# Last stage of a two-layer graph attention kernel: float32 sums per 32-node quarter in place of 128-node sums with partly split rows

## The chip, the cores and the metric

One core of a Trainium2 chip runs the whole kernel. Its engines work side by side: TensorE (PE, with weight loads shown apart as PEld), VectorE (DVE), ScalarE (ACT), GpSimd (POOL) and SyncE (SP). Each takes its own instructions in order and waits for the others by semaphores. The metric is device time in microseconds, the median of several runs. Beside it there is one profiled execution, from which all durations come.

## What is computed

Two layers of a relational graph attention network on 3125 nodes and 53125 edges, then a residual sum and a layer norm. Edges come sorted by destination. One layer, with its max taken per destination node:

```python
xr = jnp.einsum('nd,rdf->rnf', x, W)
oi = xr[etype, dst]
oj = xr[etype, src]
alpha = jax.nn.leaky_relu(oi @ q + oj @ k, NEG_SLOPE)
m = jax.ops.segment_max(alpha, dst, num_segments=n_nodes)
e = jnp.exp(alpha - m[dst])
z = jax.ops.segment_sum(e, dst, num_segments=n_nodes)
a = e / (z[dst] + EPS)
msg = (a[:, :, None] * oj.reshape(-1, heads, out_ch)).reshape(-1, heads * out_ch)
out = jax.ops.segment_sum(msg, dst, num_segments=n_nodes)
```

Layer 1 has 4 heads, layer 2 has one; rows are 768 wide. Between the layers stands an ELU; at the end `_layernorm(x + out)`. The change is in the last stage, the edge part of layer 2 with the layer norm: for each node, the sum of its edges' rows, each times its weight p = exp(alpha - m), divided by the sum of the p.

## The kernel before

A first stage makes layer 1's tables of node rows, a second does layer 1's edges and layer 2's dense products, and the last, `phase3` (L1015), layer 2's edges.

**Blocks and slots.** Edges are taken in blocks of at most 128 consecutive destination nodes and at most 2176 edges, 25 blocks (NB) in all. A block's edges lie in 17 slots (SL) of 128 edges, one edge per partition; the first block has 14 (SLF). That makes NK = 422 slots. Since edges are sorted, the edges of slot j of a block belong to a narrow stretch of its nodes, about 7.5 nodes wide, at a place near 7.5 j.

**One slot.** `gather(k)` (L1031) has POOL issue one indirect DMA (L461) that brings the 128 edges' source rows of 772 float32 into place k mod NG of the tile G; NG is 36. Column 768 and on of a row carry the constant 1 (which makes the sum of p) and the score part. `high(k)` and `low(k)` (L1134, L1151) prepare the operands of PE, `sums(k)` (L1160) adds the slot into `acc`, a PSUM tile of two halves of 386 columns, one per block, 128 nodes on the partitions.

There are two kinds of slots, chosen by `whole(k)` (L1126). A whole slot's weights of PE are `selp`, 128 edges by 128 nodes, with p where the edge goes to the node: ACT makes it in two operations (L1141, L1142), and two float32 matmuls, one per half, multiply it with the gathered rows. In the other slots ACT makes H, the rows times p rounded to the format float32r (L1146), DVE makes L, what is left (L1157), and `sel` of ones and zeros (L1148); four float32r matmuls add H and L. 281 slots are whole and 141 are split. In the last 17 slots (`late`) one of three is whole, and `sel` is made on POOL.

**Weights p of a block.** When all its rows are there: `a_alpha` (L1081) on DVE adds the scores; PE transposes them (L1098); DVE scans for the maximum of each node (L1104, L1106) and subtracts (L1109); ACT takes exp (L1113); PE transposes back (L1117); DVE puts p and its negative np in place (L1122, L1124). Ahead of this, PE spreads the block's destinations over partitions (bc, L1050), ACT copies them (sT, L1056), DVE compares (L1060, L1062), and PE picks the destinations' scores (pq, L1071).

**Order.** The program's order on every engine is written out by hand: a loop over steps k issues `gather(k)`, then `sums(k - 28)` (LAG = SL + 11), then what `ev` holds for the step, then `low(k - 26)` and `high(k - 25)`. So the sums of a block begin when its own 17 gathers and 11 more have been issued. Counted from the step of a block's first gather, `a_alpha` stands at step 19, the transposes at 20 and 23, `a_put` at 24. The end of a block (`e_y` to `e_out`, L1171 to L1217) divides, norms and stores its rows.

**Flag.** The second half of the program, a slower kernel, runs only if `flag` (L594, L1292) is not zero, which tells of inputs that the blocks can't hold. `bad` collects such cases.

Of the kernel before, what the change touches and what calls it, by code (L numbers as in the profile page):

```python
# [8 lines left out]
F32 = mybir.dt.float32  # L9
F32R = mybir.dt.float32r  # L10
# [3 lines left out]
AF = mybir.ActivationFunctionType  # L14
ALU = mybir.AluOpType
AX = mybir.AxisListType
# [4 lines left out]
P = 128  # L21
# [16 lines left out]
SL = 17  # L38
# [4 lines left out]
FRONT = 256  # L43
BACK = CAP + P + 256

WHOLE = (17, 25)


@with_exitstack
def kernel(  # L50
# [23 lines left out]
    NB = (N + P - 1) // P  # L74
# [3 lines left out]
    l1, l2 = layers  # L78
    H1 = l1["H"]
    F1 = D // H1  # L80
# [3 lines left out]
    RW = D + 4  # L84
    HW = RW // 2
    CW = F1 + 1
    LL = FRONT + E + BACK
    NK = (NB - 1) * SL + SLF
    V, S, G, T = nc.vector, nc.scalar, nc.gpsimd, nc.tensor
# [17 lines left out]
    row = keep.tile([P, P], F32, name="frow")  # L107
# [3 lines left out]
    rel3 = keep.tile([P, R, 3], F32, name="rel3")  # L111
# [6 lines left out]
    n_all = keep.tile([P, NB + 1], F32, name="n_all")  # L118
# [6 lines left out]
    bad = keep.tile([1, 2], F32, name="bad")  # L125
    oidx = keep.tile([P, 1], I32, name="oidx")
    flag = keep.tile([1, 1], I32, name="flag")
    ridx = keep.tile([P, NB, SL], I32, name="ridx")
    rfirst = keep.tile([P, len(first_rows), SL], I32, name="rfirst")
    dl = keep.tile([P, NB, SL + 1], F32, name="fdl")  # L130
# [311 lines left out]
    def base(b):  # L442

        return SLF + (b - 1) * SL if b else 0

    def slots(b):
        return SL if b else SLF

    def slot(k):

        return divmod(k - SLF + SL, SL) if k >= SLF else (0, k)

    ends = {base(b) + slots(b) - 1 for b in range(NB)}
# [65 lines left out]
    def phase1(pre, work, psum, wH, wL, qq):  # L519
# [7 lines left out]
        st = a_st  # L527
# [58 lines left out]
        def a_last():  # L586

            V.tensor_scalar(oidx, n_all[:, NB - 1:NB], col, None, op0=ALU.add)
            V.tensor_scalar(starts[0:1, 2, :NB], n_all[0:1, :NB], float(N - P), None, op0=ALU.min)
            more = work.tile([1, 2], F32, name="more", bufs=1)  # L590
            V.tensor_single_scalar(more[:, 0:1], n_all[0:1, NB:NB + 1], float(N), op=ALU.is_lt)
            V.tensor_single_scalar(more[:, 1:2], n_all[0:1, NB - 2:NB - 1], float(N - P), op=ALU.is_gt)
            V.tensor_add(bad, bad, more)
            V.tensor_add(flag, bad[:, 0:1], bad[:, 1:2])  # L594

        def a_gather(b, j):
            gathered[b, j] = gather_rows(kts[b % 3][:, j, :], kt1, b, j).ins
# [197 lines left out]
        for n in range(max(ev) + 1):  # L795
            for f, b in ev.get(n, ()):
                f(b)
            b, i = divmod(n, 6)
# [26 lines left out]
    def phase2(work, psum, wH, wL):  # L825
# [3 lines left out]
        gs = share  # L829
        NG = len(gs)  # L830
        rows = [work.tile([P, RW], F32, name=f"r2_{i}", bufs=1) for i in range(3)]
# [183 lines left out]
    def phase3(work, psum):  # L1015
        for i in range(2):
            xbs.append(work.tile([P, D], F32, name=f"xb3_{i}", bufs=1))
            x_load3(len(xbs) - 1)
        NG = 36
        gs = work.tile([P, NG, RW], F32, name="G", bufs=1)  # L1020
        als = [work.tile([P, SL + 2], F32, name=f"al2_{i}", bufs=1) for i in range(2)]
        for t in als:
# [1 line left out]
        blk = {}  # L1024
        st = {}
# [97 lines left out]
            s["np"] = work.tile([P, SL], F32, name="np2", bufs=3)  # L1123
            V.tensor_scalar(s["np"], s["pa"][:, 3 * P:3 * P + SL], -1.0, None, op0=ALU.mult)  # L1124

        def whole(k):  # L1126

            return k % 3 == 0 if late(k) else k * WHOLE[0] % WHOLE[1] < WHOLE[0]

        def late(k):  # L1130

            return k >= NK - SL

        def high(k):  # L1134
            b, j = slot(k)
            g = gs[:, k % NG, :]
            p = blk[b]["p"][:, j:j + 1]
            if whole(k):
                sel = work.tile([P, P], F32, name="selp", bufs=4)

                S.activation(sel, row, AF.Abs, bias=dl[:, b, j:j + 1], scale=-1.0)  # L1141
                S.activation(sel, sel, AF.Relu, bias=p, scale=blk[b]["np"][:, j:j + 1])  # L1142
                st[k] = [sel, g]
                return
            H = work.tile([P, RW], F32R, name="H", bufs=4)
            S.activation(H, g, AF.Copy, scale=p)  # L1146
            sel = work.tile([P, P], F32R, name="sel", bufs=4)
            (G if late(k) else V).tensor_scalar(sel, row, dl[:, b, j:j + 1], None, op0=ALU.is_equal)  # L1148
            st[k] = [sel, H]

        def low(k):  # L1151
            if whole(k):
                return
            b, j = slot(k)
            g = gs[:, k % NG, :]
            L = work.tile([P, RW], F32R, name="L", bufs=3)
            V.scalar_tensor_tensor(L, g, blk[b]["p"][:, j:j + 1], st[k][1].bitcast(F32), op0=ALU.mult, op1=ALU.subtract)  # L1157
            st[k].append(L)

        def sums(k):  # L1160
            b, j = slot(k)
            sel, *parts = st.pop(k)
            if j == 0:
                blk[b]["acc"] = psum.tile([P, 2, 512], F32, name="acc", bufs=2)
            acc = blk[b]["acc"]
            for i, a in enumerate(parts):
                for c in range(2):
                    T.matmul(acc[:, c, :HW], sel, a[:, c * HW:(c + 1) * HW], start=(j == 0 and i == 0),  # L1168
                             stop=(k in ends and i == len(parts) - 1))

        def e_y(b):  # L1171
            s = blk[b]
# [51 lines left out]
        LAG = SL + 11  # L1224
# [14 lines left out]
        for k in range(max(ev) + 1):  # L1239
            if k < NK:  # L1240
                gather(k)
            if 0 <= k - LAG < NK:
                sums(k - LAG)
            for f, a in ev.get(k, []):
                f(*a)
            if 0 <= k - LAG + 2 < NK:
                low(k - LAG + 2)
            if 0 <= k - LAG + 3 < NK:
                high(k - LAG + 3)

    with tc.manual_schedule():
        with tc.tile_pool(name="share", bufs=1) as pool:
# [4 lines left out]
            with tc.tile_pool(name="wbuf", bufs=1) as wbuf:  # L1257
                wH = wbuf.tile([P, R * DT, D + 2], F32R, name="wH")
                wL = wbuf.tile([P, R * DT, D + 2], F32R, name="wL")
                with tc.tile_pool(name="pre", bufs=1) as pre:  # L1260
                    qq = pre.tile([P, NB, H1, R], F32, name="qq")
                    with tc.tile_pool(name="work0", bufs=1) as work, tc.tile_pool(
                        name="psum0", bufs=1, space=PSUM
# [20 lines left out]
                    with tc.tile_pool(name="work1", bufs=1) as work, tc.tile_pool(  # L1284
                        name="psum1", bufs=1, space=PSUM
# [544 lines left out]
```

## Time and profile before

| what | value |
|---|---|
| median of three timed runs | 2547.97 us (2543.3 to 2552.66) |
| profiled execution, its own time | 2188.15 us |
| its span | 2186.4 us |
| mean granted clock of PE | 0.969 |
| PE busy, share of the span | 2015.1 us, 92% |
| POOL busy | 1674.3 us, 77% |
| DVE busy | 1458.8 us, 67% |
| ACT busy | 1356.5 us, 62% |
| first gather of the last stage | 1552.1 us |
| end of the last stage's gathers | 2147.6 us |
| end of its last matmul | 2174.2 us |

Times in a profile are counted from the start of the span. A group of instructions is given as line, engine, operation, tile written and tiles read, shapes and count, then busy time and mean of one in ns, then the idle time just before them on their engine and what ended most of it. A float32 matmul of the program shows up as two pairs of a weight load and a matmul instruction, a float32r matmul as one. Matmuls are pipelined, so the duration of one contains its latency; what it costs is the distance to the next.

### The profile page before, as it was taken

How to read it: one execution, taken by the hardware profiler on the slowest of the kernel's cores; microseconds unless marked ns; L12 is line 12 of the kernel's file. 1: busy time of each engine (PE TensorE's matmuls, PEld its weight loads, DVE VectorE, ACT ScalarE, POOL GpSimd, SP SyncE). 2: the span in 40 equal slices, each digit the busy share in tenths (PEclk: the TensorE clock that was granted, in tenths of full speed). 3: DMA queues.
4: the chain of work that ended last, by engine and by line, in shares of the span. 5: the costliest groups of instructions: out<-in, count | busy, mean ns of one | idle time of the engine just before them, and what ended most of it. 6: DMA issues, size and time to landing. Idle time of an engine off the chain costs nothing.

```text
span 2186.4 us, 37632 instructions
## 1 busy us (share of the span) xinstructions
PE 2015.1 (92%) x10953; PEld 1730.7 (79%) x10953; DVE 1458.8 (67%) x4031; ACT 1356.5 (62%) x3159; POOL 1674.3 (77%) x1615
## 2 busy tenths in 40 slices
PE   5979999999987799999999999999499999989997
PEld 5979998899887799999999999999355555555555
DVE  6535554454534899999999999998155555556555
ACT  5412111122111788888888888887268887878786
POOL 4257777777777888888888888886477777777774
PEclk9989999999998899999999999999799999999999
DMA  6555545545457977888787878786789998988883
GB/s 177 188 137 173 192 145 169 174 158 183 160 168 224 311 233 246 240 246 241 237 249 226 249 231 248 231 243 191 256 303 305 315 322 309 302 295 281 294 300 108
DMA packets 156842, 506.04 MB, mean 231 GB/s; under 512 B 43875, under 2 KB 57069, under 8 KB 156628
## 3 DMA queue, kind: packets, MB, share of 16 engines
q0 software_dynamic: 81904, 331.52, 49.9%
q1 hardware_dynamic: 64494, 156.04, 20.6%
q10 hardware_dynamic: 10230, 15.98, 2.2%
q8 instruction: 91, 1.49, 0.3%
q14 instruction: 123, 1.01, 0.2%
HBM read 412.55 MB, written 95.69 MB: 232 GB/s over the span
## 4 chain that ended last, share of the span: by engine, by line
PE 61%; POOL 12%; DMA 11%; issue 11%; DVE 3%; ACT 1%; POOLq 0%; SPq 0%; DVEq 0%; ACTq 0%
PE po L949 19%; PE acc L1168 14%; PE acc L894 12%; PE po L698 8%; POOL kt L461 8%; DMA G<-ftab,ridx 6%; POOL G L461 2%; DMA kt<-kt,ridx 1%; POOL share L461 1%; PE bank L282 1%; DVE L L875 1%; PE pt L260 1%; POOL sel L863 1%; PE pt L924 1%; PE po L396 1%
## 5 line engine op out<-in xcount | busy, mean ns | idle before, releaser
L861 ACT ACTIVATE H<-share,pall 128x193 fp32r<-128x193 f32 x1672 | 618.2, 447 | 104.7 <-PE acc L894 53.5
L875 DVE SCALAR_TENSOR_TENSOR L<-share,pall,H 128x193 fp32r<-128x193 f32 x1672 | 619.0, 435 | 28.2 <-issue 19.8
L949 PE MATMUL po<-wH,hT 128*128 128x386 f32 (+1 forms) x1800 | 529.1, 339 | 0.0
L461 POOL DMA_INDIRECT G<-ftab,ridx x374 | 416.0, 1112 | 113.9 <-issue 56.1
L461 POOL DMA_INDIRECT share<-ftab,ridx x374 | 437.0, 1168 | 80.4 <-DVE L L875 34.7
L461 POOL DMA_INDIRECT kt<-kt,ridx x374 | 396.3, 1060 | 114.0 <-issue 108.5
L698 PE MATMUL po<-wH,xT 128*128 128x384 f32 x1584 | 440.3, 348 | 8.8 <-ACT share L713 4.4
L1168 PE MATMUL acc<-G,selp 128*128 128x386 f32 x1124 | 417.1, 505 | 0.0
L949 PEld LDWEIGHTS po<-wH,hT 128*128 128x128 f32 x1800 | 334.1, 189 | 0.6 <-DVE hT L937 0.5
L698 PEld LDWEIGHTS po<-wH,xT 128*128 128x128 f32 x1584 | 294.6, 191 | 13.8 <-ACT share L713 6.2
L949 PE MATMUL po<-wL,hT 128*128 128x386 f32 (+1 forms) x900 | 304.8, 339 | 0.0
L1168 PEld LDWEIGHTS acc<-G,selp 128*128 128x128 f32 x1124 | 206.0, 193 | 118.7 <-issue 16.3
L698 PE MATMUL po<-wL,xT 128*128 128x384 f32 x792 | 270.3, 341 | 0.0
L894 PE MATMUL acc<-H,sel 128*128 128x386 f32 x836 | 227.0, 353 | 19.2 <-POOL sel L863 17.6
L713 ACT COPY share<-po 128x384 f32<-128x384 f32 x144 | 67.9, 478 | 275.0 <-PE po L698 268.9
L863 POOL TENSOR_SCALAR sel<-frow,fdl 128x128 fp32r<-128x128 f32 x278 | 219.0, 788 | 12.4 <-PE acc L894 1.7
L894 PE MATMUL acc<-L,sel 128*128 128x386 f32 x836 | 217.8, 342 | 0.0
L1157 DVE SCALAR_TENSOR_TENSOR L<-G,p,H 128x772 fp32r<-128x772 f32 x141 | 143.1, 1017 | 56.1 <-ACT H L1146 56.0
L894 PEld LDWEIGHTS acc<-H,sel 128*128 128x128 f32 x836 | 148.0, 190 | 36.0 <-POOL sel L863 33.7
L949 PEld LDWEIGHTS po<-wL,hT 128*128 128x128 f32 x900 | 169.6, 188 | 0.0
L894 PEld LDWEIGHTS acc<-L,sel 128*128 128x128 f32 x836 | 155.1, 191 | 0.2 <-DVE L L875 0.2
L698 PEld LDWEIGHTS po<-wL,xT 128*128 128x128 f32 x792 | 151.8, 192 | 0.0
(246 smaller groups left out, 2688.1 us busy)
## 6 DMA issues: line engine op xcount, KB each, us to landing
ftab<-share SPq DMA_DIRECT2D x75, 386.0 KB
ftab<-r SPq DMA_DIRECT2D x75, 386.0 KB
share<-in_L_gnn_W_dram SPq DMA_DIRECT2D x36, 384.0 KB
w_d<-w2hl SPq DMA_DIRECT2D x18, 768.0 KB
sT<-dr_d SPq DMA_DIRECT2D x25, 544.0 KB
share<-in_x_dram SPq DMA_DIRECT2D x25, 384.0 KB
xb_d<-share SPq DMA_DIRECT2D x25, 384.0 KB
xr<-in_x_dram SPq DMA_DIRECT2D x23, 384.0 KB
```

Of the source, the lines that this page charges most:

```text
L260: T.transpose(pt[:, f, c * P:(c + 1) * P], a[:, (2 * i + f) * P:(2 * i + f + 1) * P], ident)
L282: T.matmul(to, a[:, 2 * i + f, :], t[:, f, :w], start=(n == 0), stop=(n == 2 * DT - 1))
L461: return G.indirect_dma_start(out=to, out_offset=None, in_=tab, in_offset=_index(i[:, j:j + 1]), bounds_check=NP * R - 1, oob_is_err=False)
L698: m = T.matmul(po[:, :HALF], xT[:, s, t, :], w[:, i, sl], start=(n == 0), stop=(n == 3 * DT - 1))
L713: S.copy(to, po[:, :HALF].rearrange("p (h f) -> p h f", h=2))
L861: S.activation(H[:, c], g[:, c], AF.Copy, scale=pall[:, b, j, h:h + 1])
L863: (V if k % 3 == 0 else G).tensor_scalar(sel, row, dl[:, b, j:j + 1], None, op0=ALU.is_equal)
L875: V.scalar_tensor_tensor(L[:, c], g[:, c], pall[:, b, j, h:h + 1], H[:, c].bitcast(F32), op0=ALU.mult, op1=ALU.subtract)
L894: T.matmul(acc[:, c, :HW], sel, a[:, c * HW:(c + 1) * HW], start=(j == 0 and i == 0), stop=(k in ends2 and i == 1), skip_group_check=True)
L949: T.matmul(po[:, :wd], hT[:, k, t, :], w[:, r * DT + t, sl], start=(t == 0 and n == 0), stop=(t == DT - 1 and n == 2))
L1157: V.scalar_tensor_tensor(L, g, blk[b]["p"][:, j:j + 1], st[k][1].bitcast(F32), op0=ALU.mult, op1=ALU.subtract)
L1168: T.matmul(acc[:, c, :HW], sel, a[:, c * HW:(c + 1) * HW], start=(j == 0 and i == 0), stop=(k in ends and i == len(parts) - 1))
```

## The change

The block's 128 nodes are four quarters of 32. For each of the 17 slots a table `WINDOW` names the one or two quarters in which its edges' nodes lie (seven slots have one, ten have two). All slots are treated alike: `selp` is made for those 32 or 64 nodes alone, and each pair of slot and quarter t gets its own two float32 matmuls (one per half), with 32 weight columns, into partitions 32t to 32t+31 of `acc`. H, L, `sel` and `low` are gone.

Slots are taken in the order of `ROUNDS`, seven groups of two or three slots. A round's matmuls are issued together when its last slot's turn comes, half by half, quarter after quarter. `in_turn` maps steps to this order; gathers keep theirs. In the last 17 slots every other `selp` is made by one DVE operation in place of two of ACT's. NG is 43 in place of 36, and `selp` has 10 buffers in place of 4.

A new function `windows`, at step 17, tests on DVE (and with one small matmul) whether every edge of a block lies in its slot's window, and adds the count of those outside to `bad`; `flag` is set there and no longer in `a_last`.

```diff
-WHOLE = (17, 25)
+WINDOW = ((0,), (0,), (0,), (0, 1), (0, 1), (0, 1), (1,), (1, 2), (1, 2), (1, 2), (2,), (2, 3), (2, 3), (2, 3),
+          (2, 3), (3,), (3,))
+ROUNDS = ((3, 11), (4, 12), (5, 13), (2, 9), (0, 7, 15), (1, 8, 16), (6, 14, 10))
...
-        NG = 36
+        NG = 43
...
+        def in_turn(k):
+            b, i = slot(k)
+            o = [j for r in ROUNDS for j in r if j < slots(b)]
+            return b, o[i]
...
         def high(k):
-            b, j = slot(k)
-            g = gs[:, k % NG, :]
+            b, j = in_turn(k)
             p = blk[b]["p"][:, j:j + 1]
-            if whole(k):
-                sel = work.tile([P, P], F32, name="selp", bufs=4)
-                S.activation(sel, row, AF.Abs, bias=dl[:, b, j:j + 1], scale=-1.0)
+            lo, hi = WINDOW[j][0] * 32, WINDOW[j][-1] * 32 + 32
+            sel = work.tile([P, 64], F32, name="selp", bufs=10)[:, :hi - lo]
+            if late(k) and k % 2:
+                V.tensor_scalar(sel, row[:, lo:hi], dl[:, b, j:j + 1], p, op0=ALU.is_equal, op1=ALU.mult)
+            else:
+                S.activation(sel, row[:, lo:hi], AF.Abs, bias=dl[:, b, j:j + 1], scale=-1.0)
                 S.activation(sel, sel, AF.Relu, bias=p, scale=blk[b]["np"][:, j:j + 1])
-                st[k] = [sel, g]
+            st[b, j] = sel
+
+        def sums(k):
+            b, j = in_turn(k)
+            n = slots(b)
+            if not any(j == [i for i in r if i < n][-1] for r in ROUNDS):
                 return
-            H = work.tile([P, RW], F32R, name="H", bufs=4)
-            S.activation(H, g, AF.Copy, scale=p)
-            sel = work.tile([P, P], F32R, name="sel", bufs=4)
-            (G if late(k) else V).tensor_scalar(sel, row, dl[:, b, j:j + 1], None, op0=ALU.is_equal)
-            st[k] = [sel, H]
-
-        def low(k):
...
+            o = [(i, t) for r in ROUNDS for i in r if i < n for t in WINDOW[i]]
+            now = [(i, t) for i, t in o if i in next(r for r in ROUNDS if j in r)]
+            for c in range(2):
+                for i, t in now:
+                    u = [x for x, y in o if y == t]
+                    T.matmul(acc[32 * t:32 * t + 32, c, :HW], st[b, i][:, 32 * (t - WINDOW[i][0]):][:, :32],
+                             gs[:, (base(b) + i) % NG, c * HW:(c + 1) * HW], start=(i == u[0]), stop=(i == u[-1]))
+            for i, t in now:
+                st.pop((b, i), None)
+
+        def windows():
+            lim = work.tile([P, 2, SL], F32, name="lim", bufs=1)
+            for j in range(SL):
+                V.memset(lim[:, 0, j:j + 1], 32.0 * WINDOW[j][0])
+                V.memset(lim[:, 1, j:j + 1], 32.0 * WINDOW[j][-1] + 32.0)
...
+            V.tensor_tensor(v[0], d, lim[:, 0, None, :].to_broadcast([P, NB, SL]), op=ALU.is_ge)
+            V.tensor_tensor(v[1], d, lim[:, 1, None, :].to_broadcast([P, NB, SL]), op=ALU.is_lt)
+            V.tensor_mul(v[0], v[0], v[1])
...
+            V.tensor_reduce(out_, v[1].rearrange("p b j -> p (b j)"), AX.X, ALU.add)
+            po = psum.tile([P, 512], F32, name="bc", bufs=2)
+            T.matmul(po[:1, :1], out_, rel3[:, 1, 0:1], start=True, stop=True)
...
-            if 0 <= k - LAG + 2 < NK:
-                low(k - LAG + 2)
+            if k == SL:
+                windows()
             if 0 <= k - LAG + 3 < NK:
                 high(k - LAG + 3)
```

More of the change, by code (lines that the diff above doesn't have):

```diff
@@ L593, in a_last @@
             V.tensor_add(bad, bad, more)
-            V.tensor_add(flag, bad[:, 0:1], bad[:, 1:2])
         def a_gather(b, j):
@@ L1124, in a_put @@
             V.tensor_scalar(s["np"], s["pa"][:, 3 * P:3 * P + SL], -1.0, None, op0=ALU.mult)
-        def whole(k):
-            return k % 3 == 0 if late(k) else k * WHOLE[0] % WHOLE[1] < WHOLE[0]
         def late(k):
             return k >= NK - SL
+        def in_turn(k):
+            b, i = slot(k)
+            o = [j for r in ROUNDS for j in r if j < slots(b)]
+            return b, o[i]
         def high(k):
-            b, j = slot(k)
-            g = gs[:, k % NG, :]
+            b, j = in_turn(k)
@@ L1148, in high @@
-            (G if late(k) else V).tensor_scalar(sel, row, dl[:, b, j:j + 1], None, op0=ALU.is_equal)
-            st[k] = [sel, H]
-        def low(k):
[L1152 to L1163, printed above, removed]
+            lo, hi = WINDOW[j][0] * 32, WINDOW[j][-1] * 32 + 32
@@ new lines, in high @@
+            sel = work.tile([P, 64], F32, name="selp", bufs=10)[:, :hi - lo]
[3 more added lines that the diff above has]
+                S.activation(sel, row[:, lo:hi], AF.Abs, bias=dl[:, b, j:j + 1], scale=-1.0)
+                S.activation(sel, sel, AF.Relu, bias=p, scale=blk[b]["np"][:, j:j + 1])
+            st[b, j] = sel
[3 more added lines that the diff above has]
+            if not any(j == [i for i in r if i < n][-1] for r in ROUNDS):
+                return
+            if "acc" not in blk[b]:
@@ L1164, in sums @@
                 blk[b]["acc"] = psum.tile([P, 2, 512], F32, name="acc", bufs=2)
             acc = blk[b]["acc"]
[L1166 to L1169, printed above, removed]
+            o = [(i, t) for r in ROUNDS for i in r if i < n for t in WINDOW[i]]
+            now = [(i, t) for i, t in o if i in next(r for r in ROUNDS if j in r)]
@@ new lines, in sums @@
+            for c in range(2):
[10 more added lines that the diff above has]
+                V.memset(lim[:, 1, j:j + 1], 32.0 * WINDOW[j][-1] + 32.0)
+            own = work.tile([P, NB], F32, name="own3", bufs=1)
+            V.tensor_sub(own, n_all[:, 1:NB + 1], n_all[:, :NB])
+            v = [work.tile([P, NB, SL], F32, name=f"v{i}", bufs=1) for i in range(2)]
+            d = dl[:, :, :SL]
+            V.tensor_tensor(v[0], d, lim[:, 0, None, :].to_broadcast([P, NB, SL]), op=ALU.is_ge)
+            V.tensor_tensor(v[1], d, lim[:, 1, None, :].to_broadcast([P, NB, SL]), op=ALU.is_lt)
+            V.tensor_mul(v[0], v[0], v[1])
+            V.tensor_tensor(v[1], d, own[:, :, None].to_broadcast([P, NB, SL]), op=ALU.is_lt)
+            V.tensor_tensor(v[1], v[1], v[0], op=ALU.is_gt)
+            out_ = work.tile([P, 1], F32, name="outside", bufs=1)
+            V.tensor_reduce(out_, v[1].rearrange("p b j -> p (b j)"), AX.X, ALU.add)
+            po = psum.tile([P, 512], F32, name="bc", bufs=2)
+            T.matmul(po[:1, :1], out_, rel3[:, 1, 0:1], start=True, stop=True)
+            V.tensor_add(bad[:, 0:1], bad[:, 0:1], po[:1, :1])
+            V.tensor_add(flag, bad[:, 0:1], bad[:, 1:2])
```

## The prediction

> **What bounds the kernel now.** I read the page first, then windows over the last stage (the change touches nothing else that takes time), then its groups, then the timeline of single instructions.
>
> ```profile
> span 2186.4 us, 37632 instructions
> 1552.00:1600.00 48.00, 20.78 (x87) 10.29 (x86) 10.62 (x25) 16.12 (x33) 37.24 (x36) 0.62 0.88 296
> 1600.00:2147.60 547.60, 524.21 (x2148) 309.31 (x2147) 307.43 (x718) 452.75 (x881) 430.00 (x387) 0.98 0.90 303
> 2147.60:2186.40 38.80, 25.75 (x106) 18.43 (x104) 21.63 (x40) 22.55 (x37) 10.98 (x13) 0.89 0.07 26
> ```
>
> The columns after the length are busy us of PE, PEld, DVE, ACT and POOL, then granted clock, DMA share and GB/s. In the long middle stretch PE is busy 96%, POOL only 79%. That looks like a PE bound. The groups and the timeline correct it:
>
> ```profile
> L461 POOL DMA_INDIRECT G<-ftab,ridx x374 | 416.0, 1112 | 113.9 <-issue 56.1
> L1168 PE MATMUL acc<-G,selp 128*128 128x386 f32 x1124 | 417.1, 505 | 0.0
> L1168 PEld LDWEIGHTS acc<-G,selp 128*128 128x128 f32 x1124 | 206.0, 193 | 118.7 <-issue 16.3
> L1157 DVE SCALAR_TENSOR_TENSOR L<-G,p,H 128x772 fp32r<-128x772 f32 x141 | 143.1, 1017 | 56.1 <-ACT H L1146 56.0
> ```
>
> A gather costs 1.112 us and the idle before it is 113.9/374 = 0.305 us, the same 0.30 each time in the timeline: a gap of issue, not a wait. 422 gathers x 1.412 = 596 us, and that is the whole way from the first (1552.1) to the end of the last (2147.6). No gap among the 422 is above 0.35 us. So POOL never waits for a buffer: **the issue of gathers is the bound**, with PE close behind. What makes a gather long stands here, POOL beside DVE:
>
> ```profile
> 1795.91 1.00 POOL L461 DMA_INDIRECT G<-ftab,ridx  x1 [0.31 <-issue]
> 1797.22 1.45 POOL L461 DMA_INDIRECT G<-ftab,ridx  x1 [0.30 <-issue]
> 1798.98 1.00 POOL L461 DMA_INDIRECT G<-ftab,ridx  x1 [0.30 <-issue]
> 1796.78 1.02 DVE L1157 SCALAR_TENSOR_TENSOR L<-G,p,H 128x772 fp32r<-128x772 f32 x1 [0.40 <-ACT H L1146]
> ```
>
> L ends at 1797.80 and the gather 0.87 later: it lost what was left of L after its own first 0.13 us. Counted so over the timeline, 227 gathers with none of L, sT/oh (L1060, L1062) and p/np in progress lost 1.6 us in all over 1.00 each; the 184 beside an L lost 41.1; 11 beside the others alone lost 2.6.
>
> What PE needs, from issue to issue:
>
> ```profile
> 1702.86 2.76 PE L1168 MATMUL acc<-G,selp 128*128 128x386 f32 x8
> 1705.55 0.38 PE L1050 MATMUL bc<-d,one 1*128 1x512 bf16 x1
> 1705.87 0.62 PE L1168 MATMUL acc<-H,sel 128*128 128x386 f32 x2
> 1706.33 0.52 PE L1168 MATMUL acc<-L,sel 128*128 128x386 f32 x2
> 1706.68 1.46 PE L1168 MATMUL acc<-G,selp 128*128 128x386 f32 x4
> ```
>
> Eight float32 instructions take 2.69 us, 0.336 each; a float32 matmul is two of them (1124 for 281 slots of two matmuls), so 0.672, and a slot that is not split 1.34. A split slot takes 1705.87 to 1706.68 = 0.81. 281 x 1.34 + 141 x 0.81 = 491 us, 19.8 per block of 17 slots (422/17 = 24.8 blocks). The spreads, transposes and pq add 2.4 (four bc of 0.32, one of 0.16, pa 0.33, e 0.16, pq 0.45). 22.2 us of work in a gather period of 24.0.
>
> **The change, part by part.**
>
> *PE.* A block has 27 slot-and-quarter pairs (seven slots of one quarter, ten of two), so 54 float32 matmuls with 32 weight columns. The streamed width stays 386, so each still takes 0.672. All hangs on how far different quarters overlap, and the trace has no two matmuls in different quarters. Ends: none overlap, 54 x 0.672 = 36.3 us a block; all four do, six rounds of one pass and the last of two (quarter 2 comes twice), 8 x 2 x 0.672 = 10.8. The Trainium skill, "TensorE: Matmul & The Clock Gate", Part 3 on packing, says matmuls in different column strips run together, but start strictly in order. A matmul here is two instructions on the same quarter, so its second waits for its first, and only that second lies beside the first of the next quarter: a factor of 2, **18.1 us**, with the rest 20.5. I take this. The same section has a rule against the change: a weight load overlaps a running matmul only in other row strips, and every quarter uses all rows. By it 108 loads a block lie bare; the nearest row, the 17-column load of pa (L1098), is 0.10 us, so +10.8 and 31.3 a block. The row above speaks otherwise: 1124 full-width loads using all rows, 0.193 us each, and no idle time before their matmuls. I go by the row and keep the rule for the upper end. Changing from 32-column work to the full-width bc and back is about 8 changes each way; the present change from L to e (17 rows) costs some 0.1 us, so at most 1.6.
>
> *DVE and POOL.* 141 L and 130 sel leave DVE. With L gone the gathers lose only what sT, oh, p and np cost: some 27 gathers at the 0.26 of those without an L (7 us), and 1.6. The gathers then take 422 x 1.305 = 551 + 9 = 560 us instead of 596: 22.6 a block, above PE's 20.5, with bounds of 555 and 571. The skill's "SBUF — State Buffer", Who interferes with whom, would allow less: two-input DVE instructions hold up only POOL's reads of SBUF, and it infers that making descriptors doesn't need that. By it L would cost a gather nothing and this part would bring 0. The 184 gathers above say 41 us in the trace, so the row decides: **-36 us**.
>
> *ACT.* Now 281 x (0.391 + 0.493) + 141 x 0.927 = 379 us; afterwards 414 pairs, at full width's price 366, at 32 or 64 columns less. Not a bound. *DMA* share rises from 0.90 to 0.90 x 596/560 = 0.96: room, but a little, and landings may come later.
>
> *Buffers.* A slot's G is read only when its round ends. Counting positions, slot 1 is done at step 41 after its block's start and its buffer is gathered into at 44; slots 0 and 6 have 5 steps. Before, all had 8. Behind that gather stand all later ones in POOL's queue. PE gets to step 41 after the next block's transposes: a's inputs land 4.0 us after the last gather's end, p follows 5.7 later (4.5 to 8), now less with DVE and ACT lighter, say 5; then a round of eight matmuls, 2.7. That is 11.7, and the gather is due 0.3 + 10 x 1.305 = 13.4 after. A margin of 1.7 us; some blocks will miss it: +5 (0 to 25).
>
> *The test of windows* at step 17: 34 memsets at some 0.1 us, by the 0.15 of 1-column rows, and a few operations over 425 columns at twice the 0.31 of L1062: 8 us of DVE, between al and scan of block 0. The first sums start 8 us later; PE's slack of 2 us a block takes it up; the gathers go on. +3 (0 to 10).
>
> *Tail.* After the last gather, p comes 6.7 us later (2154.3); the last block's sums ran 2158.3 to 2174.2, 15.9 us. Now 18.1, with less left over from block 23: 0 (-6 with full overlap).
>
> Sum: -36 + 5 + 3 = **-28 us** on the profiled execution, 2188.15 (span 2186.4 and 1.75 around it), to 2160. The timed runs' median is 2547.97, 360 us above, with no trace of why. If PE is slower there, the stage is nearer PE's bound, where I save 22.2 - 20.5 = 1.7 us a block, 42 us. That is of the same size, so I carry the difference over: **2520**.
>
> **The rivals.**
> 1. *Quarters don't overlap* (slower). PE takes 36.3 + 2.4 = 38.7 us a block, 960 us in place of 596, the last block 20 more: +384, 2932. It decides below an overlap of 36.3/(24.0 - 2.4) = 1.68. For it: no row shows overlap, and float32 takes two instructions. Against: the skill's statement above, and that loads and matmuls do overlap now.
> 2. *Overlap, but loads or late rounds hold the gathers* (slower by less): bare loads in part, the margin of 1.7 us missed in most blocks, or a half clock after pauses of PE as at 1552 to 1600 (0.62). 0.3 to 2 us a block above 24.0: +8 to +50, so 2556 to 2598. All loads bare would be 33.7 a block, with rival 1.
> 3. *All four overlap*: PE 13.2 a block, POOL the bound, no misses, tail -6: -42, 2506; down to 2455 if PE is slower in the timed runs (at 0.85 of the clock the stage is now 22.2/0.85 x 24.8 = 648, and 560 after).
> 4. *No change*: gathers stay long for another reason, or savings and misses cancel: 2548.
>
> The test of windows sends the kernel into its second half only if an edge lies outside; worked out on the inputs, none does.
>
> **How the numbers follow.** Forecast 0.48 (its own range 2505 to 2538), rival 3 0.14, no change 0.06, rival 2 0.14, rival 1 0.18. Two runs differ by 0.3% (7.6 us) without a change. Faster 0.62, same 0.06, slower 0.32. The range 2455 to 2595 leaves out rival 1 and little else.
>
> **What would show it.** Right: 27 x 4 L1168 matmul instructions a block at 0.33 us from issue to issue; gathers mostly at 1.00 with 0.30 between, the last ending some 33 us sooner from the first; long ones only beside sT. Wrong: instructions 0.67 apart in pairs (rival 1), gaps over 0.35 before gathers released by PE acc (rival 2), gathers still long without L (rival 4).

## The result, and the profile after

The changed kernel takes **2717.82 us** (median of 4 runs, 2707.35 to 2727.92), the kernel before beside it 2547.74: a ratio of **1.069, interval [1.066, 1.072]**. Forecast was 2520, and the range ended at 2595.

One thing must be known before any number is read. This program has two conditions, some 360 us apart: every set of runs shows the kernel before either near 2540 us or near 2182 us, with no run between. Which one it is goes with the set of runs (each set is one stay on one chip; sets 1 and 6 below have the same chip and not the same condition). The profile of before that the prediction was read from (2188 us) is of the second condition, and the timed runs beside it and beside the change are of the first. I call them **C2540** and **C2182**. A profile of the kernel before taken in C2540 is the fair partner for the one of after; it came with the first experiment.

Windows over the last stage, in the same three parts as before (length, busy us of PE, PEld, DVE, ACT and POOL, granted clock, DMA share, GB/s). First the kernel before, in C2540:

```profile
1861.80:1909.80 48.00, 10.37 (x53) 3.65 (x52) 5.25 (x14) 7.42 (x16) 36.42 (x36) 0.50 0.88 304
1909.80:2502.90 593.10, 537.71 (x2142) 310.26 (x2143) 304.90 (x714) 454.64 (x879) 419.95 (x386) 0.97 0.84 279
2502.90:2551.40 48.50, 36.23 (x145) 25.59 (x143) 27.61 (x54) 32.36 (x56) 10.93 (x12) 0.91 0.07 26
```

Then the changed kernel, in C2540:

```profile
span 2718.5 us, 39134 instructions
1856.40:1904.40 48.00, 5.80 (x29) 1.58 (x28) 4.26 (x43) 4.47 (x9) 37.01 (x37) 0.50 0.89 303
1904.40:2684.80 780.40, 537.72 (x3125) 148.08 (x3126) 172.21 (x485) 404.05 (x1025) 389.18 (x386) 0.81 0.64 212
2684.80:2718.50 33.70, 19.02 (x183) 8.50 (x181) 10.51 (x34) 16.73 (x40) 1.02 (x1) 0.88 0.10 37
```

And the changed kernel in C2182, from a later experiment:

```profile
1548.50:1596.50 48.00, 17.42 (x111) 5.10 (x113) 12.05 (x63) 14.50 (x37) 37.33 (x36) 0.57 0.88 298
1596.50:2110.60 514.10, 353.39 (x3068) 115.60 (x3062) 164.01 (x466) 395.68 (x1004) 396.46 (x387) 0.82 0.93 322
2110.60:2144.40 33.80, 18.29 (x160) 7.72 (x160) 10.49 (x34) 13.80 (x34) 1.03 (x1) 0.75 0.10 37
```

The stage begins at almost the same time in C2540 (1861.8 before, 1856.4 after), so the whole difference of 167 us between the two spans is made here: gathers 641.1 to 828.4 us (+187.3), what follows them 48.5 to 33.7 (-14.8), and the 5.4 us of the start. No engine is busy longer: POOL is down from 420 to 389 us, DVE from 305 to 172, PE is level, in a stretch that is 187 us longer. Somebody waits. The groups, first the gather of the kernel before in C2540 (L461), then the sums (L1166, middle stretch) and the gather (L464) of the changed kernel in C2540:

```profile
L461 POOL DMA_INDIRECT G<-ftab,ridx x374 | 406.1, 1086 | 161.3 <-issue 85.2 <-PE acc L1168 40.4 <-remote 13.4
L1166 PE MATMUL acc<-G,selp 128*32 128x386 f32 x2506 | 472.4, 579 | 141.7 <-issue 137.0 <-ACT sd L1216 2.8 <-ACT selp L1149 0.9
L464 POOL DMA_INDIRECT G<-ftab,ridx x374 | 377.1, 1008 | 368.2 <-PE acc L1166 159.3 <-PE bc L1052 105.0 <-issue 100.4
```

The gather has come down from 1086 to 1008 ns, in the direction that was forecast. But the idle time before it is 368 us in place of 161, and 264 us of it (159.3 + 105.0) ended with PE, 40 before: POOL waits for places to gather into. Where, the timeline of POOL shows over one block (start, duration, then idle before it):

```profile
2117.97 1.01 POOL L464 DMA_INDIRECT G<-ftab,ridx  x1 [0.30 <-issue]
2119.28 1.01 POOL L464 DMA_INDIRECT G<-ftab,ridx  x1 [0.30 <-issue]
2128.22 1.01 POOL L464 DMA_INDIRECT G<-ftab,ridx  x1 [7.93 <-PE bc L1052]
2132.74 1.00 POOL L464 DMA_INDIRECT G<-ftab,ridx  x1 [3.51 <-PE acc L1166]
2134.05 1.01 POOL L464 DMA_INDIRECT G<-ftab,ridx  x1 [0.31 <-issue]
```

It is the same two in every block: gathers 9 and 10 (counted from 0), which take the places of slots 0 and 1 of the block before last, the ones with 5 and 3 steps of margin. 47 gathers of 422 wait, 274 us together (beyond the usual 0.30): 44 of them are these two, some 11.5 us per block, and 19 us is one wait in the third block, of which more below. In the kernel before, in C2540, 54 gathers wait 57 us in all. The difference, 217, less the 30 us that shorter gathers save (the excess over 1.00 us fell from 34.4 to 4.2), is the +187.

Why the places are not free, PE's timeline of the same block shows:

```profile
2104.11 1.79 PE L1166 MATMUL acc<-G,selp 128*32 128x386 f32 x16
2106.13 0.37 PE L1052 MATMUL bc<-d,one 1*128 1x512 bf16 x1 [0.22 <-issue]
2106.84 0.82 PE L1166 MATMUL acc<-G,selp 128*32 128x386 f32 x2 [0.35 <-issue]
2108.27 0.81 PE L1166 MATMUL acc<-G,selp 128*32 128x386 f32 x3 [0.60 <-issue]
...
2119.68 0.80 PE L1166 MATMUL acc<-G,selp 128*32 128x386 f32 x1 [1.32 <-issue]
2121.10 0.83 PE L1166 MATMUL acc<-G,selp 128*32 128x386 f32 x1 [0.61 <-issue]
2122.51 2.73 PE L1166 MATMUL acc<-G,selp 128*32 128x386 f32 x8 [0.58 <-issue]
2125.18 0.60 PE L1052 MATMUL bc<-d,one 1*128 1x512 bf16 x1
2125.71 0.82 PE L1100 MATMUL pa<-fident,al 128*17 128x128 f32 x3
2126.46 1.51 PE L1166 MATMUL acc<-G,selp 128*32 128x386 f32 x16
2127.90 0.23 PE L1052 MATMUL bc<-d,one 1*128 1x128 bf16 x1
2130.82 0.23 PE L1119 MATMUL pa<-fident,e 17*128 17x17 f32 x1 [2.70 <-ACT e L1115]
2130.98 1.50 PE L1166 MATMUL acc<-G,selp 128*32 128x386 f32 x15
```

The row at 2126.46 shows what the change can do: 16 matmul instructions in 1.5 us, four quarters at once. Before it PE crawls. For 16 us, from 2106.1 to 2122.5, its instructions start on a grid of 0.71 us (0.71, 1.42, 2.1 apart), a few at a time, and it waits for nothing that the profile shows ("issue"). I call this **step mode**. It is not the half clock: the granted clock is 1.00 until 2116.2, ten us into the steps, and 0.50 from there to 2126.5. Counting as a stretch three or more such distances between PE's starts (starts within 0.12 us taken as one, breaks of up to 3 us allowed), the last stage of the change has 26 in C2540, about one per block, at the end of a block's matmuls, and none in C2182. Behind the steps in PE's queue stand the next block's transposes (L1100, L1119), and behind each of these one of the two rounds that free the places: the round at 2126.46 lets gather 9 go, the one at 2130.98 gather 10. So p of a block is put in place 23.4 us (median) after the block's last gather.

Step mode is not PE's alone. At the start of the stage the test of windows runs on DVE, and after some 19 of its 34 memsets, 0.03 us apart, DVE falls onto the same grid:

```profile
1884.27 0.06 DVE L1176 MEMSET lim<- 128x1 f32 x1 [1.34 <-issue]
1885.00 0.06 DVE L1175 MEMSET lim<- 128x1 f32 x1 [0.67 <-issue]
1886.40 0.06 DVE L1176 MEMSET lim<- 128x1 f32 x1 [1.34 <-issue]
```

From the first memset to `flag` it takes 36.2 us here, and 28 to 36 in all six profiles of changed forms in C2540; in all nine in C2182 it takes 5.4 to 5.6. The scan of block 0 stands behind it, so the first sums start late: that is the wait of 19 us above.

In C2182 the same code shows no step mode, and PE waits for the scores, as one wants it to:

```profile
1901.50 1.50 PE L1166 MATMUL acc<-G,selp 128*32 128x386 f32 x12
1902.93 0.39 PE L1052 MATMUL bc<-d,one 1*128 1x512 bf16 x1
1912.06 0.80 PE L1100 MATMUL pa<-fident,al 128*17 128x128 f32 x3 [8.75 <-DVE al L1095]
1912.79 2.80 PE L1166 MATMUL acc<-G,selp 128*32 128x386 f32 x16
1915.60 0.23 PE L1119 MATMUL pa<-fident,e 17*128 17x17 f32 x1
```

### The profile page after: what moved, and what is told of

It reads as the page before. It is cut to its first block, busy times and chain, and to the rows that moved or that the text cites. A ratio compares the mean times of both kernels' runs of the same rounds, so it can differ in the third digit from the quotient of the medians.

```text
span 2718.5 us, 39134 instructions
## 1 busy us (share of the span) xinstructions
PE 2145.3 (79%) x11951; PEld 1626.5 (60%) x11951; DVE 1309.9 (48%) x3810; ACT 1287.8 (47%) x3282; POOL 1611.9 (59%) x1604
## 4 chain that ended last, share of the span: by engine, by line
PE 46%; ACT 14%; another core or an unknown queue 13%; issue 12%; DVE 3%; POOL 2%; DMA 1%; POOLq 0%; DVEq 0%; ACTq 0%; SPq 0%
PE po L700 16%; PE po L951 16%; PE acc L896 10%; ACT selp L1149 5%; ACT selp L1148 3%; PE acc L1166 2%; ACT sT L1058 2%; ACT L1115 1%; ACT L1216 1%; POOL share L464 1%; DVE L L877 1%; PE px L677 1%; PE pt L926 1%; ACT share L1228 1%
## 5 line engine op out<-in xcount | busy, mean ns | idle before, releaser
L464 POOL DMA_INDIRECT kt<-kt,ridx x374 | 392.8, 1050 | 400.5 <-DVE lim L559 279.6
L1166 PE MATMUL acc<-G,selp 128*32 128x386 f32 x2684 | 490.6, 573 | 142.7 <-issue 138.0
L700 PE MATMUL po<-wH,xT 128*128 128x384 f32 x1584 | 508.1, 384 | 112.9 <-issue 91.8
L464 POOL DMA_INDIRECT G<-ftab,ridx x374 | 377.1, 1008 | 368.2 <-PE acc L1166 159.3
L464 POOL DMA_INDIRECT share<-ftab,ridx x374 | 432.5, 1156 | 80.5 <-issue 37.6
L700 PEld LDWEIGHTS po<-wH,xT 128*128 128x128 f32 x1584 | 332.9, 216 | 148.6 <-issue 117.5
L1166 PEld LDWEIGHTS acc<-G,selp 128*32 128x32 f32 x2684 | 123.3, 119 | 422.8 <-issue 396.8
L700 PE MATMUL po<-wL,xT 128*128 128x384 f32 x792 | 299.9, 379 | 44.6 <-issue 44.3
L1058 ACT CAST sT<-bc 128x512 bf16<-128x512 f32 (+1 forms) x125 | 63.0, 508 | 361.5 <-remote 348.4
L700 PEld LDWEIGHTS po<-wL,xT 128*128 128x128 f32 x792 | 170.6, 215 | 70.8 <-issue 70.8
L1149 ACT ACTIVATE selp<-selp,p,np 128x64 f32<-128x64 f32 (+1 forms) x413 | 177.1, 429 | 14.8 <-DVE np L1126 1.1
```

Of the source, the lines that this page charges most:

```text
L464: return G.indirect_dma_start(out=to, out_offset=None, in_=tab, in_offset=_index(i[:, j:j + 1]), bounds_check=NP * R - 1, oob_is_err=False)
L700: m = T.matmul(po[:, :HALF], xT[:, s, t, :], w[:, i, sl], start=(n == 0), stop=(n == 3 * DT - 1))
L1058: S.copy(s["sT"][:, 4 * i * P:4 * i * P + n], bc[:, :n])
L1166: T.matmul(acc[32 * t:32 * t + 32, c, :HW], st[b, i][:, 32 * (t - WINDOW[i][0]):][:, :32], gs[:, (base(b) + i) % NG, c * HW:(c + 1) * HW], ...
```

## The experiments

Waits are the gathers' idle times over 0.35 us, each less the usual 0.30, summed; stage is from the first gather to the end of the last; clock is the granted clock over the stage. Six sets of runs, each beside the kernel before on the same chip:

| set | kernel | before | ratio [interval] | stage us | waits us | clock |
|---|---|---|---|---|---|---|
| 1, C2540 | before again | 2540.7 | 0.999 [0.997, 1.001] | 641.1 | 57 | 0.93 |
| 1 | all slots whole | 2540.7 | 1.000 [0.998, 1.002] | 636.1 | 78 | 0.96 |
| 1 | slot by slot | 2540.7 | 1.003 [1.002, 1.005] | 637.6 | 78 | 0.95 |
| 1 | low slots first | 2540.7 | 1.010 [1.007, 1.013] | 682.7 | 128 | 0.80 |
| 2, C2182 | before, 31 places | 2183.9 | 0.999 [0.997, 1.001] | 595.2 | 0 | 0.95 |
| 2 | pairs | 2183.9 | 0.980 [0.977, 0.982] | 561.1 | 0 | 0.83 |
| 2 | first quarter only | 2183.9 | 0.983 [0.978, 0.987] | 564.0 | 0 | 0.96 |
| 3, C2540 | the change again | 2541.0 | 1.066 [1.063, 1.069] | 827.1 | 272 | 0.77 |
| 3 | pairs | 2541.0 | 1.016 [1.012, 1.021] | 699.2 | 144 | 0.79 |
| 3 | before, 31 places | 2541.0 | 0.998 [0.996, 1.000] | 638.2 | 59 | 0.94 |
| 3 | slot by slot | 2541.0 | 1.007 [1.003, 1.010] | 640.6 | 81 | 0.95 |
| 4, C2182 | slot order | 2180.7 | 0.980 [0.976, 0.984] | 561.2 | 0 | 0.80 |
| 4 | two tiles | 2180.7 | 0.983 [0.979, 0.987] | 561.3 | 0 | 0.95 |
| 5, C2182 | the change again | 2185.3 | **0.982 [0.978, 0.987]** | 562.1 | 0 | 0.80 |
| 5 | slot order | 2185.3 | 0.979 [0.975, 0.982] | 562.0 | 0 | 0.80 |
| 5 | two tiles | 2185.3 | 0.983 [0.980, 0.987] | 561.6 | 0 | 0.95 |
| 6, C2182 | slot order | 2177.9 | 0.983 [0.979, 0.986] | 562.5 | 0 | 0.79 |
| 6 | two tiles | 2177.9 | 0.984 [0.980, 0.987] | 562.5 | 0 | 0.94 |

**Before again (no edit).** Which condition do the timed runs have?

> The kernel before, unchanged, for a second profile of it. In the profile of the changed kernel the first stage, in which no line of work is changed, runs from 122 to 994 us; in the profile of before that the prediction used, from 124 to 699. Theory S (the first profile of before is not what its timed runs look like): the span is near 2546 us, the kt gathers end near 990, and PE's starts show steps of 0.71 us there. Theory P (the change lengthens the first stage, by way of the longer PE program): the span is near 2190 and the kt gathers end near 700.

The timed runs have C2540, and this profile with them: its span is 2551.4 us. Of the 365 us over the first profile, 297 are there when the first stage's gathers end (995.1 in place of 698.6): PE, working on layer 1's tables, has 22 stretches of step mode there (none in C2182) and a clock of 0.80 (126 to 995 us) in place of 0.98 (126 to 698). The second stage has none, although PE is denser there than anywhere (busy 807 of the 830 us from 1020 to 1850, clock 0.99). The last stage is 46 us longer, also without step mode on PE. It begins with a stop: ACT and DVE stand for 21.7 and 23.9 us until 1912.7, for something that the profile can't name. So p of block 1 comes 28 us after its last gather (12 in C2182). PE, busy 96% of this stage in C2182, doesn't make that up: p stays at 20.3 us (median) after a block's last gather, where it was 9.4.

**All slots whole.** The part of the change that drops H and L, alone:

```diff
-            return k % 3 == 0 if late(k) else k * WHOLE[0] % WHOLE[1] < WHOLE[0]
+            return True
```

> The kernel before with every slot whole: 128-column float32 products, no H, L and sel. One part of the change alone (no split of rows), without quarters and rounds. PE's price is 1.34 us a slot, 22.8 + 2.4 = 25.2 us a block, so 625 us for the stage. If what costs is in the quarters and rounds, this lies within 30 us of the kernel before (+29 by PE's price, some of it back by freed gathers). If the lack of the split itself costs (ACT's two operations per slot on PE's path), it is slower by over 100 us, like the change.

Gathers lose only 8.0 us over 1.00 each (34.4 in the kernel before beside it), so what made them long went with L and `sel`; but PE, with 17 x 1.34 us of sums per block, now paces them, and the waits are 78 us in place of 57. No change in time.

**Slot by slot.** The change with the same matmuls, but safe margins and no rounds:

```diff
-ROUNDS = ((3, 11), (4, 12), (5, 13), (2, 9), (0, 7, 15), (1, 8, 16), (6, 14, 10))
+ROUNDS = tuple((j,) for j in range(17))
```

> The changed kernel with one slot a round, in the order of the gathers: as many matmuls, but each slot's sums stand at its own step, and a buffer of G is gathered into 15 steps later instead of 3 to 10. Less overlap of quarters (two at most). Theory M (the margin: gathers wait for rounds that end too late): POOL's waits for PE go, and the time falls by over 100 us, below 2600. Theory I (PE itself is slow to issue the longer program, in steps of 0.71 us): the stage stays near 830 us and the time near 2717, since the number of PE's instructions is the same.

Nearly the whole loss is gone, and with it PE's step mode in this stage (no stretch). The number of PE instructions is the same, so neither the 108 loads a block nor the matmuls with 32 columns cost the 170 us: rounds do. A late p alone does not cost it either: here p comes 30.9 us after a block's last gather, later than the 23.4 in the change, but the places are freed in the order in which gathers need them. It is no gain: PE needs about as long as before, since neighbouring slots share quarters and overlap at most two at a time.

**Low slots first.** Rounds of three, with a least margin of 5:

```diff
-ROUNDS = ((3, 11), (4, 12), (5, 13), (2, 9), (0, 7, 15), (1, 8, 16), (6, 14, 10))
+ROUNDS = ((0, 7, 15), (1, 8, 16), (2, 9), (3, 11), (4, 12), (5, 13), (6, 14, 10))
```

> The changed kernel with the same seven rounds, in the order of their first slots: slot 0's buffer now has 13 steps, slot 1's 11, and the least margin is 5 (slot 6) where it was 3 (slot 1). Overlap of quarters and the number of instructions stay. Theory M: the waits of gathers for PE shrink by half or more and the time falls by 60 us or more. Theory I: within 20 us of 2717.

Only the order of the rounds differs. Half of the waits go (274 to 128 us), and with them most of the loss in time: 1.010 in place of 1.069. The step mode stays (22 stretches, clock 0.80). So the order of the rounds and step mode are two things, and both count.

**Before, with 31 places.** A margin of 3 without the change:

```diff
-        NG = 36
+        NG = 31
```

> The kernel before with 31 places in G in place of 36: a buffer is gathered into 3 steps after its sums' step, as slot 1's is in the changed kernel, where before it was 8. Nothing else moves. If a margin of 3 is enough by itself to make gathers wait for PE, the kernel gets slower by 50 to 180 us (2 to 7 us a block). If the margin matters only together with the rounds or with a PE that stops, it stays within 20 us.

It cost nothing there. In C2540 again:

> The kernel before with 31 gather buffers instead of 36, so that the least margin is 3, again. Where the kernel before takes 2184 it cost nothing (0.9993). Where it takes 2540: theory M+S expects the same 0.99 to 1.01 if the last stage shows few 0.71-us steps, since the round of p comes early enough; theory M alone expects 1.03 or more.

Nothing there either, 59 us of waits against 57. The small margin alone is harmless in both conditions (p comes 13.5 us after the last gather here); the theory that margins cost by themselves falls.

**Pairs.** The change with two slots to a round from 0 up, least margin 8 as before:

```diff
-ROUNDS = ((3, 11), (4, 12), (5, 13), (2, 9), (0, 7, 15), (1, 8, 16), (6, 14, 10))
+ROUNDS = ((0, 7), (1, 8), (2, 9), (3, 11), (4, 12), (5, 13), (6, 14), (10, 15, 16))
```

> The changed kernel with eight rounds of two slots (the last of three), low slots first: three or four quarters still overlap, and the least margin is 8 steps (slot 6) in place of 3. By the margin alone the stage should come near the gathers' own 560 us or at least under 640, so 2470 to 2540, faster than both kernels. If PE's steps of 0.71 us, which run e4 kept (and runs e1 and e2 did not have in the last stage), are what is left in e4, they stay and the time stays at 2550 to 2570.

In C2182 a gain of 2%: no gather waits, and 422 gathers take 561.1 us, nearly the bare 1.00 + 0.30 each. In C2540:

> The change with its slots taken in pairs from 0 up, so that the least margin is 8 as in the kernel before, again, beside the change itself. Theory M+S and theory M: gathers wait for nothing, last stage near 561 us as in the run before, ratio 0.98 where the kernel before takes 2184 and 0.98 to 0.99 where it takes 2540 (the 50 us are the same, over a longer time). If the steps of TensorE hold the stage by themselves, ratio over 1.00 where it takes 2540.

1.016. Even with the old margins PE comes late (15 stretches of step mode, p 24.7 us after the last gather): waits of 144 us, now spread over gathers 10 to 15. Low slots first, with a least margin of 5, has 128. So the least margin is no measure of the loss by itself.

**First quarter only.** The slot-by-slot form (its `ROUNDS` too) without the products of each slot's second quarter from the second block on. It leaves these edges out of the sums, and PE has 34 float32 matmuls a block in place of 54:

```diff
-            o = [(i, t) for r in ROUNDS for i in r if i < n for t in WINDOW[i]]
+            o = [(i, t) for r in ROUNDS for i in r if i < n for t in (WINDOW[i][:1] if b else WINDOW[i])]
```

> Run e2 (one slot a round) with the products of each slot's second quarter left out after the first block: the sums lack these edges. PE has 34 matmuls a block instead of 54 and must wait for its operands, while no more than one or two quarters overlap. If PE's steps of 0.71 us come where PE has run into waits, they show in the last stage (ten stretches or more, granted clock below 0.87) although PE has the least to do, and the stage stays above 600 us. If they come from four quarters at once, there are none, and the stage falls to 560 to 590 us, so 2465 to 2500.

It fell on C2182, where PE holds nothing up in any form: 564 us with 17 products a block, 561 to 562 with 27. It shows that PE is no bound any more there, and tells nothing about step mode.

**The change again, in both conditions.** This is the test of the whole explanation.

> The changed kernel again, beside the three runs below on one chip. Two conditions are known by the time of the kernel before: about 2184 us (stage 1's gathers end near 700 us, no 0.71-us steps) or about 2540 us (they end near 995 us, with the steps). Theory M+S (the small margins of slots 0 and 1 and TensorE's 0.71-us steps are jointly the cause): where the kernel before takes 2184, the change is a gain, ratio 0.98 to 1.00, and POOL waits for gathers 9 and 10 for less than 3 us per block; where it takes 2540, ratio 1.06 to 1.07 as measured first. Theory M alone (the margins cost by themselves): ratio 1.06 or more on both. Theory C (the change brings the steps itself in the last stage, whatever stage 1 does): ratio 1.03 or more even where the kernel before takes 2184.

Set 3 was C2540: 1.066, with 272 us of waits. Then, in C2182:

> The changed kernel a third time, beside the two runs below. Where the kernel before takes about 2180 us: theory M+S expects 0.98 to 1.00; theory M alone (margins) or C (the change brings its steps whatever stage 1 does) 1.03 or more. Where it takes 2540: 1.066 again, and then the two runs below decide between theories T and R.

**0.982**: the change is a gain there, with the tight margins and all. Its gathers, last stage:

```profile
L464 POOL DMA_INDIRECT G<-ftab,ridx x374 | 384.0, 1027 | 114.0 <-issue 102.7 <-DMA G<-ftab,ridx 4.6 <-PE acc L1166 2.1
```

114.0/374 is 0.305 again: not one gather waits over 0.35 us. The theories that blame the margins alone, or the change's own matmuls alone, fall here.

**Slot by slot again**, in C2540:

> The change with each slot in a round of its own, from 0 up, again beside the change: where the kernel before takes 2540 it gave 1.0034. Where it takes 2184, a PE that runs without steps leaves it no wait: ratio 0.98 to 0.99, as its cut-down form gave 0.9826; if the column tiles of three slots matter to the time, 1.00 or more, and then more than the change itself.

The result of set 1 repeats.

**Slot order.** To see whether four quarters at once bring the step mode, the products of one slot were put one after another within the rounds of the change:

```diff
-            for c in range(2):
-                for i, t in now:
+            for j, c in [(j, c) for j in dict(now) for c in range(2)]:
+                for i, t in [(i, t) for i, t in now if i == j]:
```

> The change with the same rounds, but in each round the products of one slot follow each other, first half and second half of its columns, before the next slot's come: the same number of matmuls and loads, started by the same gathers, with two column tiles at once at most in place of four. Theory T (TensorE's 0.71-us steps at half clock come from four column tiles at work at once): no stretch of steps per block in the last stage, its granted clock back over 0.90, and gathers 9 and 10 wait little; but TensorE needs some 22 + 5 us per block, so a last stage of 640 to 700 us, ratio 1.00 to 1.03 where the kernel before takes 2540. Theory R (the steps come from the rounds, a pause and then some 48 instructions in a row): the steps stay, clock near 0.80, ratio 1.07 or more.

The edit didn't do what it was made for. PE's timeline of this kernel still has four quarters at once:

```profile
1900.99 1.52 PE L1166 MATMUL acc<-G,selp 128*32 128x386 f32 x16
1902.45 0.39 PE L1052 MATMUL bc<-d,one 1*128 1x512 bf16 x1
```

16 instructions in 1.46 us, as in the change, and the starts stand in groups of four within 40 ns: products of the later slot start beside those of the earlier one although they are written behind them. The records do not name the quarter, so whether the program's order was kept up to the engine is not shown. This run separates nothing. Two more runs met C2182 as well:

> The change with its rounds but the products of one slot after another (two column tiles at once at most), again. Where the kernel before takes 2180: 0.98 again. Where it takes 2540: theory T (four tiles at once bring the steps) 1.00 to 1.03 with a granted clock over 0.90 in the last stage and no stretch of steps per block; theory R (bursts bring them) 1.06 or more with a clock near 0.80.

> The change with its rounds but the products of one slot after another (two column tiles at once at most), once more. On a chip where the kernel before takes 2540 (the open case): theory T (four tiles at once bring the long stretches of steps) 1.00 to 1.03 and a granted clock over 0.90 in the last stage; theory R (rounds of many instructions in a row bring them; its clock of 0.80 where the kernel before takes 2180 speaks for it) 1.06 or more with a clock near 0.80. On a chip where it takes 2180: 0.98 again, which tells nothing new.

**Two tiles.** Slots of one quarter in pairs, the others alone, so that mostly two quarters are at work at once (1070 groups of starts in the trace are of two, 159 of three or four; the second edit lets a round be empty in the short first block):

```diff
-ROUNDS = ((3, 11), (4, 12), (5, 13), (2, 9), (0, 7, 15), (1, 8, 16), (6, 14, 10))
+ROUNDS = ((0, 6), (3,), (1, 10), (4,), (2, 15), (5,), (7,), (8,), (9,), (11,), (12,), (13,), (14,), (16,))
...
-            if not any(j == [i for i in r if i < n][-1] for r in ROUNDS):
+            if not any([j] == [i for i in r if i < n][-1:] for r in ROUNDS):
```

> The change with slots in rounds of one or two, so chosen that never more than two column tiles work at once: slots of one quarter are paired (0 with 6, 1 with 10, 2 with 15), the others go alone; every slot's buffer is free early enough. TensorE's time per block falls against the slot-by-slot form by its three pairs (3 x 1.3 us). Theory T: no steps in the last stage, clock over 0.90, gathers wait less than the 78 to 81 us of the slot-by-slot form, ratio 0.98 to 1.00 where the kernel before takes 2540 and about 0.98 where it takes 2184. If the number of matmuls or their rounds bring the steps: as the pairs, 1.016 or more where it takes 2540.

> Small rounds, at most two column tiles at once, safe margins, again. Where the kernel before takes 2180: 0.983 again. Where it takes 2540: theory T 0.98 to 1.00, no steps; otherwise as the pairs, 1.016 or more.

> Small rounds, at most two column tiles at once, safe margins, once more. On a chip where the kernel before takes 2540: theories T and R both expect no long stretches of steps, clock over 0.90, ratio 0.98 to 1.00; if the number of matmuls brings them, 1.016 or more. On a chip where it takes 2180: 0.983 again.

The same gain as the change in C2182, at a clock of 0.94 to 0.95 and not 0.80. That clock difference goes through all sets, in both conditions: forms with three or four quarters at once (the change, low slots first, pairs, slot order) 0.77 to 0.83, forms with one or two 0.94 to 0.96. In C2182 it costs nothing, since PE has time. Whether the two-tile form is a gain in C2540 could not be seen, as none of its three runs fell there; it is the one that I would try next.

## Why the prediction was wrong

**The step that failed is the carry-over**, "That is of the same size, so I carry the difference over". It took a sum made on a profile of one condition to runs of another, and in the other one the term **Buffers**, "+5 (0 to 25)", is 217 us (waits of 274 against 57). The mechanism stood in the working as it came: slots 0 and 1, a round behind the next block's transposes, a gather due 13.4 us after the last one and the round done at 11.7. What was wrong is the 9 us for p after the last gather. In C2540 it is 23.4 in the change, and was 20.3 in the kernel before; the trace in hand showed 9.4. A p that late costs little where the low slots are summed first (1.010, p at 21.5) or in turn (1.003 and 1.007, p at 30.9); it costs 6.6 to 6.9% where slots 0 and 1 stand in the fifth and sixth round. Rival 2 had this mechanism, at 8 to 50 us. The gap of 360 us between profile and runs was the sign; I named it ("with no trace of why") and went on as if the same waits held. A slower PE was priced by its work alone; priced as a later p as well, it would have used up the margin of 1.7 us.

The other steps can be judged in C2182, for which the sum was made: -28 forecast, -38.4 measured (2146.95 against 2185.30).

- *DVE and POOL*, -36: **right**. The gathers take 562.1 us in place of 595.5, forecast 560. With L gone their excess over 1.00 us is 11.8 us where it was 45.3. The other reading, that an L costs a gather nothing, does not hold: in all the forms without L the excess is 4 to 14 us.
- *PE*: **mis-sized**, on the safe side for the change. I took a factor of 2, 18.1 us a block, since the second instruction of a float32 matmul was to hold up the next quarter, by the rule of strict order in the Trainium skill, "TensorE: Matmul & The Clock Gate", Part 3. The trace shows 16 instructions per 1.43 us, so eight such groups make 11.4 us a block: four at once, as in rival 3, whose 10.8 was close. The rule against the change, loads that overlap only in other row strips, doesn't show either: no such time lies between the groups. (The 33.7 us a block for bare loads under rival 1 counts the 2.4 of spreads and transposes twice; it is 31.3.) For the kernel before, the work of 22.2 us in 24.0 was too small: PE stood idle only 23.4 us in the 547.6 of the middle stretch, 1.0 a block and not 1.8.
- *Buffers*, +5: in C2182 nothing, no gather waits; p comes 10.2 us after the last gather, near the 9 I took.
- *Test of windows*, +3: nothing in C2182, where it took 5.5 us and no gather moved. In C2540 it took 36.2 and made the wait of 19 us.
- *Tail*, 0 (or -6 with full overlap): 33.8 us after the last gather in place of 38.8, -5, which goes with the full overlap.

In C2540 the first of these holds too (excess 34.4 to 4.2), and so does the overlap; it is step mode together with the order of the rounds, not PE's work, that makes the loss.

**Shown**: the two conditions; that the change gains 1.8% in one and loses 6.6 to 6.9% in the other; that the loss is POOL waiting for the places of slots 0 and 1; that the order of the rounds alone takes the waits from 274 to 128 us and the ratio from 1.069 to 1.010, that pairs leave 144 us, and that the slot-by-slot form, without step mode on PE in the last stage, loses only 0.3 to 0.7%.

**Not shown**: what step mode is and why it comes in C2540 only; what sets it off; and whether any form is faster than the kernel before in C2540. None of those tried there is.

Three simple triggers of step mode do not fit. Four quarters at once are not needed: DVE's memsets and the first stage step without them. A dense PE is not enough: the second stage has no stretch. And the fetching of code gives no pattern: fetches of 16 KB (queue q8) take about 1 us in both conditions, and stretches begin anywhere from 0 to 37 us after one. That forms with fewer quarters at once have no steps on PE in the last stage is seen in C2540 for slot by slot alone; whether the quarters or the pause and burst of the big rounds matter there is open.

## What to carry to other kernels

Where a profile's own time and the timed runs differ by more than their spread, the profile is of another condition: no difference worked out on it may be carried over before every margin is priced with the late engine of the other one. A margin of a few steps has to be priced with the most delayed engine that frees it; order the work so that the place needed first is freed first, even where the sums don't ask for it. And overlap that makes an engine faster than its neighbour needs buys nothing: in the condition where all was well, forms with half of the overlap took the same time.

## What the runs showed of the hardware

- **Float32 products for 32 columns each in different quarters of the output overlap fourfold**, both instructions of each: 16 instructions of 386 columns in 1.43 us, where one alone takes 0.336. In nine of ten groups the four starts lie within 40 ns, and the groups 0.33 us apart. The form written slot after slot shows the same groups.
- **A two-input DVE operation over 772 columns goes with longer issues of indirect DMAs on POOL**: 1.112 us in the mean over the gathers in the kernel before, with 41.1 of the 45.3 us of excess beside an L; 1.01 to 1.03 in all forms without L.
- **A core can fall into steps of 0.71 us**, PE and DVE alike, with nothing to wait for: 22 stretches on PE in the first stage of the kernel before and 26 in the last stage of the change (the one shown lasts 16 us), all in C2540. The one shown begins at full clock, and half clock follows ten us later. 34 memsets and nine small operations on DVE took 36.2 us so, and 5.5 without. The same kernel before takes 360 us longer in C2540 than in C2182, 297 of them in the first stage.
- **A pause brings the half clock without steps.** In C2182 the clock is 0.50 from 1905.9 to 1916.1 us, over the 8.75 us of waiting shown above and 4 us of work behind it; the 16 instructions at 1912.79 take 2.7 us, 1.43 at full clock.
